# Layer 1's transposed input by way of DRAM and 32x32 transposes on VectorE instead of TensorE transposes, with its input channels in a crossed order

## The chip, the cores and the metric

The kernel runs on one core of one Trainium2 chip. A core has a matrix engine (TensorE, PE in the profile), a vector engine (VectorE, DVE), an activation engine (ScalarE, ACT), a general engine (GpSimd, POOL) and a sync engine (SP) that only issues transfers; all take their instructions in a fixed order of their own and wait for one another by semaphores. The metric is the device time of one execution in microseconds (us), lower is better. All data is 32-bit float.

## The reference

Two layers over an input `x` of 2 batches x 4096 tokens x 512 channels. Both have the same outer form: layer norm, two branches on the normalised input, both added to `x`.

```python
xn = _layernorm(x)                                  # layer 0
x = x + _L0_attn_ref(xn, ...) + _L0_ffn_ref(xn, ...)
xn = _layernorm(x)                                  # layer 1
x = x + _L1_attn_ref(xn, ...) + _L1_ffn_ref(xn, ...)

# _L0_attn_ref: x1 = xn @ w1.T; depthwise conv, silu, a state-space scan over tokens;
#               (scan * silu(xn @ v1.T)) @ w2.T
# _L0_ffn_ref:  xn and weight rounded to a 6-bit grid in blocks of 32, then xd @ wd.T
# _L1_attn_ref (linear attention):
q = relu(x @ Wq.T + bq); k = relu(x @ Wk.T + bk); v = x @ Wv.T + bv
kv = einsum('bnhd,bnhp->bhdp', k, v); k_sum = k.sum(axis=1)
out = (q @ kv) / max(q . k_sum, eps);  y = out + x;  layernorm(y) * gamma + beta
# _L1_ffn_ref, with x_prev = x one token earlier:
xr = mu_r*x + (1-mu_r)*x_prev;  xk = mu_k*x + (1-mu_k)*x_prev
sigmoid(xr @ W_r.T) * (square(relu(xk @ W_k.T)) @ W_v.T)
```

The products q, k, r and k of layer 1 contract over the channels of the normalised input. TensorE contracts over partitions, so that input must lie with channels on partitions ("transposed"), while layer norm and the values `v` use it with tokens on partitions.

## The kernel before, in words

Tokens are worked in blocks of T = 512, each of TJ = 4 tiles of 128 tokens; a batch has NB = 8 blocks, the two batches NK = 16. The program has four stages. **Stage A** (all 16 blocks) makes layer 0's two projections and the convolution. **The recurrence** runs the scan in chunks. Then for each batch come a **mixed stage** (function `mixed`, line 528), which ends layer 0 and begins layer 1, and the **layer-1 stage** (`layer1`, line 691).

In the mixed stage, `x1_of(i)` (line 576) makes the output of layer 0 for block i, called x1 here: for each tile four matmuls of the rounded branch (`branch`, line 570) and four with `w2` (line 587) go into one PSUM bank `po`, VectorE adds it to `x` (line 595), SP writes the tile to DRAM (`xd1`, line 596) for the layer-1 stage, and after the fourth tile the layer-norm scale and shift of the block stand in `mvs` (lines 600 and 601). Then for block i the loop at line 625 does the following: ScalarE writes the normalised tile `xn` (line 628); `x1_of(i + 1)` runs; sixteen TensorE transposes (four to a tile, `transposed`, line 130) go to the PSUM banks tagged `tr` and ScalarE copies them to `xnT`, channels on partitions (line 644); then for each tile a product with `wk` (line 648) into a bank tagged `mm`, VectorE's bias add (line 650), ScalarE's Relu (line 651), and one product later `summed` (line 603): `xn` against k, four matmuls of 512 columns, summed over the batch in four banks tagged `acc`. `xnT` of all eight blocks stays in SBUF for the layer-1 stage; its column 0 is the last token of the block before, copied by GpSimd (line 641).

Beside this, `gate` (line 564) loads and prepares the input `z` of block i + 2 (two transfers, a 32x32-block transpose and a multiplication on VectorE per quarter), and `quantised` (line 361) rounds tiles for the branch of later blocks: a load, four ScalarE rescales, five VectorE passes, two GpSimd passes, a VectorE transpose. `tick` (line 548) steps a clock once per tile of `x1_of` and once per tile of the k loop; it decides at which of these the four steps of a `quantised` tile are written into the program. These loads and the tiles of `gate` share eight buffers of the pool `yv`. `spread_out` (line 284) is used in stage A: it writes a block's scale and shift to DRAM and reads them back by four small transfers, so that partition 32q + p holds the values of tokens 32h + p, for all h.

The order in which an engine gets its instructions is not the order of the source: a scheduler places them when the program is built. In the built program the transposes of a block stand just ahead of its first product with `wk`.

Of the kernel before, what the change touches and what calls it, by code (L numbers as in the profile page):

```python
# [2 lines left out]

# [6 lines left out]
F32 = mybir.dt.float32  # L10
# [6 lines left out]
P = 128  # L17
D = 512
CC = D // P
T = 512  # L20
# [22 lines left out]
def block_kernel(ctx: ExitStack, tc: tile.TileContext, a: dict, out: bass.AP):  # L43
# [25 lines left out]
    q_d = dram.tile([CC, QC, L, NS, L], F32, name="q_d")  # L69
    a_d = dram.tile([CC, QC, L, NS], F32, name="a_d")  # L70
    sd = dram.tile([NK, P, TJ, 2], F32, name="sd")

    def bank(tag="mm", bufs=2):
        return ps.tile([P, D], F32, tag=tag, name=f"p_{tag}", bufs=bufs)
# [46 lines left out]
    def rescaled(dst, src, mv):  # L121
        nc.scalar.activation(dst, src, AF.Identity, bias=mv[:, 0:1], scale=mv[:, 1:2])  # L122

    def as_scale_and_bias(mv):

        nc.vector.scalar_tensor_tensor(
            mv[:, :, 0], mv[:, :, 0], -1.0, mv[:, :, 1], ALU.mult, ALU.mult
        )

    def transposed(dst, src, tag="tr"):  # L130

        pt = bank(tag).rearrange("p (c t) -> p c t", t=P)
        for cc in range(CC):
            nc.tensor.transpose(pt[:, cc, :], src[:, cc * P : (cc + 1) * P], ident)  # L134
        nc.scalar.copy(dst, pt)  # L135
# [14 lines left out]

    def laid_normalised(y, n, j):

        for h in range(QC):
            part = y.rearrange("p (c h q) -> p c h q", h=QC, q=QB)[:, :, h, :]
            rescaled(part, part, mvi[:, h, n, j, :])

    def mx_scaled(y):

# [120 lines left out]
        layernorm_stats(lambda j: xts[j], mv0[:, n])  # L281
        as_scale_and_bias(mv0[:, n])

    def spread_out(n):

        nc.sync.dma_start(out=sd[n], in_=mv0[:, n])
        for q in range(QC):
            nc.sync.dma_start(
                out=mvi[q * QB : (q + 1) * QB, :, n],
                in_=sd[n].rearrange("(h p) j k -> p h j k", p=QB),  # L290
            )

    def first_turned(work, xts):

        xnT = work.tile([P, CC, T], F32, tag="xnT", name="xnT")
# [14 lines left out]
    def turned(work, n, xi):  # L310
        xnT = work.tile([P, CC, T], F32, tag="xnT", name="xnT")
        for j in range(TJ):
            laid_normalised(xi[:, j, :], n, j)
            nc.vector.transpose(
                xnT[:, :, j * P : (j + 1) * P], xi[:, j, :].rearrange("p (c t) -> p c t", t=P)
            )
        return xnT
# [43 lines left out]
    def quantised(n, j, dst, temp):  # L361

        xq = yv.tile([P, D], F32, tag="yv", name="xq")
        nc.sync.dma_start(out=xq, in_=a["xi"][n * TJ + j])
        yield
        laid_normalised(xq, n, j)
        scales = mx_scaled(xq)
        yield
        mx_rounded(xq, scales, temp())
        yield  # L370
        nc.vector.transpose(dst().rearrange("p c t -> p (c t)"), xq)  # L371
        yield
# [155 lines left out]
    def mixed(b, z0, xds, xnTs, mvs, w2, wk):  # L528

        pg = []  # L530
        ksum = stay.tile([P, D], F32, tag="ksum", name="ksum", bufs=1)
        zs, xts, later, pos = {0: z0}, {}, [], {}
        ahead = len(xds)
        def xd_of(m, j):
            if m not in xds:
                xd = t8((P, TJ, CC, P))
                xds[m] = [xd[:, jj] for jj in range(TJ)]
            return xds[m][j]


        clock = [-2 * TJ]
        quants = [
            (2 * TJ * (m - 2) + 2 * j - 2, quantised(b * NB + m, j, partial(xd_of, m, j), t2q))
            for m in range(ahead, NB)
            for j in range(TJ)
        ]

        def tick():
            for start, q in reversed(quants):
                for t in range(start, start + 4):  # L550
                    if t == clock[0] or (t < clock[0] == -2 * TJ):
                        next(q)
            clock[0] += 1

        def x_of(i):
            xts[i] = cl.tile([P, TJ, D], F32, tag="x", name="x")
            for j in range(TJ):
                nc.sync.dma_start(out=xts[i][:, j, :], in_=tokens(x_in, b * NB + i, j))

        def flush():  # L560
            if later:
                later.pop()()

        def gate(i, cc):
            if i < NB:
                if cc == 0:
                    zs[i] = t8()
                gated(b, i, zs[i], cc)

        def branch(i, j, po):  # L570
            for k in range(CC):
                nc.tensor.matmul(  # L572
                    po, lhsT=xds[i][j][:, k, :], rhs=wd[:, k, :], start=(k == 0), stop=False
                )

        def x1_of(i):

            xt, z = xts[i], zs.pop(i)
            for j in range(TJ):
                if i in pos:  # L580
                    po = pos[i][j]
                else:
                    po = bank()
                    branch(i, j, po)
                flush()
                for k in range(CC):
                    nc.tensor.matmul(  # L587
                        po,
                        lhsT=z[:, k, j * P : (j + 1) * P],
                        rhs=w2[:, k, :],  # L590
                        start=False,
                        stop=(k == CC - 1),
                    )
                nc.gpsimd.tensor_tensor(xt[:, j, :], xt[:, j, :], b_out, ALU.add)
                nc.vector.tensor_tensor(xt[:, j, :], xt[:, j, :], po, ALU.add)  # L595
                nc.sync.dma_start(out=xd1[b * NB + i, :, j, :], in_=xt[:, j, :])
                tick()
                if i == 0:
                    gate(1, j)
            layernorm_stats(lambda j: xt[:, j, :], mvs[:, i])  # L600
            as_scale_and_bias(mvs[:, i])

        def summed(i, j, xn, kt):
            first, last = i == 0 and j == 0, i == NB - 1 and j == TJ - 1
            if first:
                pg.extend(acc() for _ in range(CC))
                nc.gpsimd.tensor_copy(ksum, kt)
            else:
                nc.gpsimd.tensor_tensor(ksum, ksum, kt, ALU.add)
            for c in range(CC):  # L610
                nc.tensor.matmul(  # L611
                    pg[c], lhsT=xn[:, j, c * P : (c + 1) * P], rhs=kt, start=first, stop=last
                )

        x_of(0)
        x_of(1)
        for i in range(ahead):

            pos[i] = [bank(("mm", "tr")[i]) if j < 2 else acc() for j in range(TJ)]
            for j in range(TJ):  # L620
                branch(i, j, pos[i][j])
                if i == 0:
                    tick()
        x1_of(0)
        for i in range(NB):
            xn = t8((P, TJ, D))
            for j in range(TJ):
                rescaled(xn[:, j, :], xts[i][:, j, :], mvs[:, i, j, :])
            if i + 2 < NB:
                x_of(i + 2)  # L630
            if i + 1 < NB:
                x1_of(i + 1)
            if i < NB - 1:
                xnT = big.tile([P, CC, T + 1], F32, tag="xnT", name="xnT")
            else:
                wide = single.tile([P, CC * (T + 1)], F32, name="wide")
                xnT = wide.rearrange("p (c t) -> p c t", t=T + 1)
            if i == 0:
                nc.gpsimd.memset(xnT[:, :, 0:1], 0.0)
            else:  # L640
                nc.gpsimd.tensor_copy(xnT[:, :, 0:1], xnTs[-1][:, :, T : T + 1])
            xnTs.append(xnT)
            for j in range(TJ):
                transposed(xnT[:, :, 1 + j * P : 1 + (j + 1) * P], xn[:, j, :])
            for j in range(TJ):
                tj = slice(1 + j * P, 1 + (j + 1) * P)
                pk = bank()
                product(pk, lambda k: xnT[:, k, tj], lambda k: wk[:, k, :])
                kt = t2("k")
                nc.vector.tensor_tensor(kt, pk, bk, ALU.add)  # L650
                nc.scalar.activation(kt, kt, AF.Relu)  # L651
                flush()
                later.append(lambda i=i, j=j, xn=xn, kt=kt: summed(i, j, xn, kt))
                gate(i + 2, j)
                tick()
        flush()
        gt = t8((P, CC, D))
        for c in range(CC):
            nc.scalar.copy(gt[:, c, :], pg[c])
        return gt, ksum  # L660
# [119 lines left out]
    with tc.tile_pool(name="tab", bufs=1) as tab:  # L780
# [3 lines left out]
        with pool("a", 2) as work, pool("pm", 1) as pm:  # L784
# [9 lines left out]
            xnT = first_turned(work, xts.pop(0))  # L794
            xts[1] = fetched(work, 1)
            measured(1, xts.pop(1))
            spread_out(1)
            xts[2] = fetched(work, 2)
            spread_out(0)
            d_ssm = column("D_ssm")  # L800
            abar, cb, b_ssm = (column(s, NS) for s in ("A", "C_ssm", "B_ssm"))
            a32 = const.tile([P, CC, L // 2], F32, name="a32")
# [16 lines left out]
            for n in range(NK):  # L819
# [4 lines left out]
                before, x1 = x1, projected(work, n, xnT, x1)  # L824
                if n + 2 < NK:
                    measured(n + 2, xts.pop(n + 2))
                    spread_out(n + 2)
                if n + 1 < NK:
                    xnT = turned(work, n + 1, xi)
                if 0 < n < NK - 1:  # L830
# [127 lines left out]
```

## Time and profile before

| | us |
|---|---|
| median of 3 runs (2497.35 to 2502.07) | 2498.64 |
| profiled execution, device time | 2500.6 |
| its span in the profile | 2498.5 |
| stage A and recurrence, up to about | 618 |
| mixed stage, batch 0, first product with `wd` to last `summed` | 618 to 1083 |
| layer-1 stage, batch 0 | 1083 to about 1557 |
| mixed stage, batch 1, its stretch in the table of stretches | 1560 to 2060 |
| layer-1 stage, batch 1 | 2060 to the end |

The profile comes from one execution. Its page gives for each engine the busy time and its share of the span; a view of the timeline lists stretches of equal instructions with their start, length and, in brackets, the idle time ahead of them and what ended it. A full-size matmul (128x128 by 128x512) appears as two passes on PE. A pass is listed as 592 ns, but the next one starts 0.43 us after it: passes overlap, so what a group of matmuls costs is read from the distance of starts, not from the sum of durations. A transpose of 128x128 is one pass.

### The profile page before, as it was taken

Reading aid. Unit: us, or ns where it says so; the run is one execution under the profiler, and the core shown is the slowest. Engines: PE = TensorE matmul, PEld = TensorE weight load, DVE = VectorE, ACT = ScalarE, POOL = GpSimd, SP = SyncE. Lnnn points to the kernel's source line nnn. Section 1 sums busy time; section 2 is a strip of 40 time slices with the busy share of each in tenths; the row PEclk is TensorE's granted clock in tenths of the full one; section 3 lists DMA queues with packets and bytes.
Section 4 is the critical chain, followed back from the end, with each engine's and each line's share of the span. In section 5 each row is a group of like instructions: output and inputs, shape, how many; then the busy total and the mean of one; then the engine's idle time right before and its main releaser. Section 6 shows DMA issues by size and latency. Waiting matters only on the chain. (4 is left out here: it accounts for less than half of the span.)

```text
span 2498.5 us, 21002 instructions
## 1 busy us (share of the span) xinstructions
PE 2444.7 (98%) x6752; PEld 1155.7 (46%) x6752; DVE 1354.6 (54%) x2796; ACT 905.5 (36%) x1668; POOL 457.7 (18%) x447
## 2 busy tenths in 40 slices
PE   7999999999999999999999999999999999999999
PEld 3444443566444444444444444444444444444444
DVE  7857465664775545126555558755542126555554
ACT  5776654444322222133333342222221133333332
POOL 1000011221443322111100003433330111100100
PEclk9999999999999999999999999999999999999999
DMA  7646332677632221101000124432220110000110
GB/s 239 214 129 213 119 117 93 180 236 249 243 114 90 84 85 68 51 33 39 34 34 34 38 72 140 157 110 91 84 85 34 51 36 36 34 34 34 38 39 25
DMA packets 168621, 239.66 MB, mean 96 GB/s; under 512 B 41408, under 2 KB 74176, under 8 KB 165440
## 3 DMA queue, kind: packets, MB, share of 16 engines
q1 hardware_dynamic: 157856, 204.77, 25.0%
q10 hardware_dynamic: 10656, 33.56, 3.4%
q8 instruction: 54, 0.88, 0.1%
q14 instruction: 55, 0.45, 0.1%
HBM read 153.77 MB, written 84.51 MB: 95 GB/s over the span
## 5 line engine op out<-in xcount | busy, mean ns | idle before, releaser
L611 PE MATMUL p_acc<-k,t 128*128 128x512 f32 x512 | 232.3, 597 | 9.2 <-ACT k L651 9.2
L140 PE MATMUL p_acc<-xnT,w_v_w 128*128 128x512 f32 x512 | 226.1, 599 | 7.8 <-ACT x L335 7.8
L750 POOL TENSOR_TENSOR x<-x,row_beta 128x512 f32<-128x512 f32 x64 | 87.8, 1372 | 794.0 <-ACT xn L122 794.0
L140 PE MATMUL p_acc<-w_W_r,t 128*128 128x512 f32 x512 | 232.8, 593 | 0.0
L140 PE MATMUL p_acc<-xnT,w_w_w 128*128 128x512 f32 x512 | 226.6, 601 | 5.8 <-DVE mv L118 5.0
L140 PE MATMUL p_mm<-t,w_W_k 128*128 128x512 f32 x512 | 222.3, 592 | 0.0
L140 PE MATMUL p_acc<-w_W_v,t 128*128 128x512 f32 x512 | 222.3, 592 | 0.0
L737 DVE TENSOR_SCALAR den<-p_tr 128x8 f32<-128x8 f32 x128 | 18.4, 151 | 348.3 <-PE p_tr L729 348.1
L140 PE MATMUL p_mm<-w_Wk,xnT 128*128 128x512 f32 x448 | 203.5, 597 | 1.6 <-DVE x L595 1.6
L587 PE MATMUL p_mm<-w_w_w,t 128*128 128x512 f32 x448 | 201.1, 592 | 0.0
L140 PE MATMUL p_mm<-xnT,w_Wq 128*128 128x512 f32 x448 | 194.8, 592 | 0.0
L572 PE MATMUL p_mm<-w_d,t 128*128 128x512 f32 x416 | 187.1, 592 | 0.2 <-DVE x L595 0.2
L122 ACT ACTIVATE xq<-xq,mvi 128x128 f32<-128x128 f32 x256 | 105.3, 482 | 204.3 <-DMA xq<-in_xi 157.4
L140 PEld LDWEIGHTS p_acc<-xnT,w_v_w 128*128 128x128 f32 x512 | 98.2, 192 | 133.1 <-issue 120.0
L140 PEld LDWEIGHTS p_acc<-xnT,w_w_w 128*128 128x128 f32 x512 | 98.4, 193 | 131.5 <-issue 121.0
L611 PEld LDWEIGHTS p_acc<-k,t 128*128 128x128 f32 x512 | 97.4, 191 | 133.2 <-issue 120.2
L140 PEld LDWEIGHTS p_mm<-t,w_W_k 128*128 128x128 f32 x512 | 97.3, 190 | 122.5 <-issue 122.2
L140 PEld LDWEIGHTS p_acc<-w_W_v,t 128*128 128x128 f32 x512 | 97.1, 190 | 121.5 <-issue 113.1
L383 DVE SCALAR_TENSOR_TENSOR xc<-x,col_conv_w,xc 128x512 f32<-128x512 f32 x128 | 92.3, 769 | 106.5 <-POOL x L325 95.3
L650 DVE TENSOR_TENSOR k<-p_mm,row_bk 128x512 f32<-128x512 f32 x64 | 43.7, 684 | 182.3 <-PE p_mm L140 182.3
L587 PEld LDWEIGHTS p_mm<-w_w_w,t 128*128 128x128 f32 x448 | 85.1, 190 | 107.1 <-issue 106.9
L140 PEld LDWEIGHTS p_mm<-xnT,w_Wq 128*128 128x128 f32 x448 | 84.8, 189 | 107.7 <-issue 107.2
(168 smaller groups left out, 3413.8 us busy)
## 6 DMA issues: line engine op xcount, KB each, us to landing
x<-in_x SPq DMA_DIRECT2D x126, 256.0 KB, 4.4
vd<-v ACTq DMA_DIRECT2D x64, 256.0 KB, 2.7
cd<-xs SPq DMA_DIRECT2D x64, 256.0 KB, 2.7
xq<-in_xi SPq DMA_DIRECT2D x64, 256.0 KB, 4.1
xg<-cd SPq DMA_DIRECT2D x16, 1024.0 KB, 7.9
v<-vd SPq DMA_DIRECT2D x64, 256.0 KB, 4.0
xd<-x SPq DMA_DIRECT2D x64, 256.0 KB, 2.3
x<-xd SPq DMA_DIRECT2D x16, 1024.0 KB, 4.7
```

Source lines behind the costliest of these rows:

```text
L122: nc.scalar.activation(dst, src, AF.Identity, bias=mv[:, 0:1], scale=mv[:, 1:2])
L140: nc.tensor.matmul(out_ap, lhsT=lhsT(k), rhs=rhs(k), start=(k == 0), stop=(k == CC - 1))
L383: nc.vector.scalar_tensor_tensor(xc, x1[:, cc, tap : tap + T], conv_w[:, cc, tap : tap + 1], xc, ALU.mult, ALU.add,)
L572: nc.tensor.matmul(po, lhsT=xds[i][j][:, k, :], rhs=wd[:, k, :], start=(k == 0), stop=False)
L587: nc.tensor.matmul(po, lhsT=z[:, k, j * P : (j + 1) * P], rhs=w2[:, k, :], start=False, stop=(k == CC - 1),)
L611: nc.tensor.matmul(pg[c], lhsT=xn[:, j, c * P : (c + 1) * P], rhs=kt, start=first, stop=last)
L650: nc.vector.tensor_tensor(kt, pk, bk, ALU.add)
L737: nc.vector.tensor_scalar(den, pc[:, :, P:], EPS_DEN, None, ALU.max)
L750: nc.gpsimd.tensor_tensor(xt[:, j, :], xt[:, j, :], beta, ALU.add)
```

## The change

The normalised x1 with channels on partitions is made without TensorE. `turned_x1(i, j)` reads the tile that was written to `xd1` back from DRAM, in four transfers of 32 partitions x 4 pieces of 128 channels, so that partition 32q + p of the buffer `y1` holds the tokens 32h + p (h = 0 to 3), of each the channels 128q to 128q + 127. Scale and shift of a token now differ by h, so ScalarE rescales `y1` in place with four instructions of 128 columns, taking the values from `mvj`, which is laid out like `y1` by `spread_out` (now a general function: one small write, four small reads per block). One VectorE transpose of 32x32 blocks writes the tile into `xnT`. Row 32q + k of chunk g of `xnT` is then channel 128q + 32g + k rather than 128g + 32q + k: a crossed order. The rows of Wq, Wk, W_r and W_k and the vectors mu_r and mu_k are laid out on the host in this order, at no cost on the device.

`xn` with tokens on partitions is still made, for `summed`. The step "load" of tile j of block i is put at tick 8i + j, which is in `x1_of(i + 1)`, and "rescale and transpose" two ticks later (the last block: four ticks earlier). `tick` now takes its steps from a table of events. The product with `wk` takes its bank from the tag `tr`, which the transposes have left, rather than `mm`. `y1` takes buffers of the pool `yv`, whose number stays eight. `transposed` remains for the first block of stage A.

```diff
+    sd1 = dram.tile([NK, P, TJ, 2], F32, name="sd1")
...
+    def spread_out(dst, via, mv):
+
+        nc.sync.dma_start(out=via, in_=mv)
+        for q in range(QC):
+            nc.sync.dma_start(
+                out=dst[q * QB : (q + 1) * QB], in_=via.rearrange("(h p) j k -> p h j k", p=QB)
+            )
...
+        clock, events = [-2 * TJ], defaultdict(list)
         def tick():
-            for start, q in reversed(quants):
-                for t in range(start, start + 4):
-                    if t == clock[0] or (t < clock[0] == -2 * TJ):
-                        next(q)
+            for do in events.pop(clock[0], ()):
+                do()
             clock[0] += 1
...
+        def xnT_of(i):
...
+        def turned_x1(i, j, mvj):
+            y = yv.tile([P, D], F32, tag="yv", name="y1")
+            for q in range(QC):
+                nc.sync.dma_start(
+                    out=y[q * QB : (q + 1) * QB].rearrange("p (h m) -> p h m", h=QC),
+                    in_=xd1[b * NB + i, :, j].rearrange("(h p) (q m) -> q p h m", h=QC, q=QC)[q],
+                )
+            yield
+            for h in range(QC):
+                part = y[:, h * P : (h + 1) * P]
+                rescaled(part, part, mvj[:, h, j, :])
+            nc.vector.transpose(
+                xnT_of(i)[:, :, 1 + j * P : 1 + (j + 1) * P].rearrange(
+                    "p g (h t) -> p h g t", h=QC
+                ),
+                y.rearrange("p (h g k) -> p h g k", h=QC, g=QC),
+            )
+            yield
...
             as_scale_and_bias(mvs[:, i])
+            mvj = stay.tile([P, QC, TJ, 2], F32, tag="mvj", name="mvj")
+            spread_out(mvj, sd1[b * NB + i], mvs[:, i])
+
+            for j in range(TJ):
+                turn = turned_x1(i, j, mvj)
+                start = 2 * TJ * i + j - (TJ if i == NB - 1 else 0)
+                at(start, partial(next, turn))
+                at(start + 2, partial(next, turn))
...
-            for j in range(TJ):
-                transposed(xnT[:, :, 1 + j * P : 1 + (j + 1) * P], xn[:, j, :])
+            xnT = xnTs[i]
             for j in range(TJ):
                 tj = slice(1 + j * P, 1 + (j + 1) * P)
-                pk = bank()
+                pk = bank("tr")
                 product(pk, lambda k: xnT[:, k, tj], lambda k: wk[:, k, :])
...
+    crossed = lambda v: v.reshape(QC, QC, QB, -1).transpose(1, 0, 2, 3).reshape(D, -1)
+    turned_crossed = lambda v: crossed(v.T)
...
-        "Wq": ("L1_attn_Wq", turned),
+        "Wq": ("L1_attn_Wq", turned_crossed),
```

## The prediction

> **What bounds the kernel now.** I read the page's busy times first:
>
> ```profile
> PE 2444.7 (98%) x6752; PEld 1155.7 (46%) x6752; DVE 1354.6 (54%) x2796; ACT 905.5 (36%) x1668; POOL 457.7 (18%) x447
> ```
>
> TensorE is the bound; nothing else is over 54%. Work taken off PE counts in full, provided what replaces it never makes PE wait. Next, the table of stretches for the two mixed stages, which the change touches (columns: stretch, length, then busy us and instructions of PE, PEld, DVE, ACT, POOL, the granted clock, DMA share, GB/s):
>
> ```profile
> 660.00:1112.00 452.00, 438.24 (x1113) 200.25 (x1113) 214.27 (x424) 114.85 (x224) 129.28 (x118) 0.99 0.24 82
> 1560.00:2060.00 500.00, 494.40 (x1275) 227.04 (x1274) 215.95 (x455) 116.48 (x224) 129.45 (x117) 1.00 0.24 81
> ```
>
> There VectorE has half its time free, ScalarE three quarters, the DMA engines three quarters. Third, PE's timeline around the sixteen transposes of block 1, which stands for the steady blocks:
>
> ```profile
> 733.56 3.60 PE L587 MATMUL p_mm<-w_w_w,t 128*128 128x512 f32 x8
> 737.00 1.04 PE L134 MATMUL p_tr<-ident,t 128*128 128x128 f32 x8
> 738.27 0.65 PE L134 MATMUL p_tr<-ident,t 128*128 128x128 f32 x4 [0.24 <-ACT xnT L135]
> 738.76 1.02 PE L140 MATMUL p_mm<-w_Wk,xnT 128*128 128x512 f32 x2
> 739.63 0.60 PE L134 MATMUL p_tr<-ident,t 128*128 128x128 f32 x4
> 740.06 6.17 PE L140 MATMUL p_mm<-w_Wk,xnT 128*128 128x512 f32 x14
> 746.07 3.60 PE L611 MATMUL p_acc<-k,t 128*128 128x512 f32 x8
> ```
>
> From 737.00 to 746.07 are 9.07 us with sixteen transposes and sixteen passes of `wk`. Eight full passes take 3.43 us from start to start (733.56 to 737.00), sixteen 6.87. The transposes with their one wait are worth **2.20 us a block**. Last, the stalls at the head of a batch, where VectorE has the rounding of several tiles at once:
>
> ```profile
> 672.17 1.12 PE L134 MATMUL p_tr<-ident,t 128*128 128x128 f32 x4 [5.31 <-ACT xnT L135]
> ...
> 699.60 3.70 PE L611 MATMUL p_acc<-k,t 128*128 128x512 f32 x8 [3.18 <-ACT k L651]
> ...
> 709.00 3.70 PE L611 MATMUL p_acc<-k,t 128*128 128x512 f32 x8 [2.27 <-ACT k L651]
> ...
> 1619.42 3.70 PE L140 MATMUL p_mm<-w_Wk,xnT 128*128 128x512 f32 x8 [1.59 <-DVE x L595]
> ...
> 1625.45 5.40 PE L611 MATMUL p_acc<-k,t 128*128 128x512 f32 x8 [2.32 <-ACT k L651]
> ```
>
> **Removed: 256 transposes.** [...] But transposes overlap as other passes do: 2.20 us for sixteen is 0.1375 us each, and the sum is 256 x 0.1375 = **35.2 us**. [...]
>
> **Added.** The rows nearest to the new operations:
>
> ```profile
> L122 ACT ACTIVATE xq<-xq,mvi 128x128 f32<-128x128 f32 x256 | 105.3, 482 | 204.3 <-DMA xq<-in_xi 157.4 <-DVE x L595 17.4 <-DMA y<-yd 7.5
> L314 DVE STREAM_TRANSPOSE xnT<-xi 128x512 f32<-128x512 f32 x60 | 38.6, 684 | 6.1 <-PE p_acc L140 3.1 <-ACT xi L122 2.9
> L390 DVE STREAM_TRANSPOSE xs<-xc 128x512 f32<-128x512 f32 x64 | 60.6, 1035 | 0.9 <-ACT xc L387 0.7
> L135 ACT COPY xnT<-p_tr 128x512 f32<-128x512 f32 x58 | 32.6, 587 | 241.3 <-PE p_tr L134 241.3
> ```
>
> - VectorE: 64 transposes. Runs of 32 elements as in L314: 0.69 us; every element apart as in L390: 1.04. I take 0.69, the nearer form: 44 us over both stages, 2.8 a block.
> - ScalarE: four rescales a tile; four of L122 take 1.65 us in the timeline, against 0.54 from start to start for the copy that goes (two in 1.08). 1.1 us more a tile, 71 us in all; ScalarE goes from 25% to about 32% of the stages, VectorE from 45% to 50%.
> - Transfers: 16.8 MB more. The nearest row for pieces of 512 bytes is `xg`, 1 MB in 7.9 us, so 16 x 7.9 = 126 us of DMA over some 950 us: from a quarter busy to under 40%.
> - SP issues per block 16 loads at 0.36 us (as `xg`), one small write at 0.34 and four small reads at 0.43: 7.8 us in 55. The twenty that it issues per block now take about as long. Each `y1` load waits for its tile of `xd1` to land (2.3 us). Behind it stand the next tile's `xd1` write, whose data comes 6.9 us later, and loads of `xq` a block ahead of need.
>
> All this lies beside PE, unless one chain is late. **The added wait** is the scale and shift by way of DRAM:
>
> ```profile
> xg<-cd SPq DMA_DIRECT2D x16, 1024.0 KB, 7.9
> ...
> xd<-x SPq DMA_DIRECT2D x64, 256.0 KB, 2.3
> ...
> mvi<-sd SPq DMA_DIRECT2D x64, 4.0 KB, 1.8
> ...
> sd<-mv SPq DMA_DIRECT2D x16, 4.0 KB, 2.7
> ```
>
> As the changed program is built, ScalarE's rescales of block m stand in its queue among the Relus of block m-1, and VectorE's first two transposes of block m among the bias adds. So a late `mvj` holds up k of the block before. I lay it on the block whose last `w2` pass ends at 851.28. `mvs` is ready 3.7 us later (L126 at 854.78); write issued and landed: 6.7; four reads issued: 8.4; landed: 10.2; sixteen rescales: 16.8; the third k's Relu behind them: 17.4. PE meanwhile has the products of tiles 0 and 1 with up to half a branch (8.6), `summed` 0 (12.0), product 2 (15.4), `summed` 1 (18.9), product 3 (22.3), and then `summed` 2, which needs that Relu. **Slack 4.9 us**: hidden. `xnT` itself is not late: tiles 0 and 1 are turned a block ahead; tiles 2 and 3 right after the first two bias adds, about 8 us before their products. The last block is turned during the k loop of block 6: its first product comes 24.9 us after its `x1` ends, the chain takes about 13.
>
> **Moved.** The products with `wk` go to the `tr` banks: `po` and `pk` no longer share two banks, which removes the 1.59 us at 1619.42. GpSimd's copy of column 0 moves ahead, into `x1_of`; behind it stand the products of the rounding, and GpSimd is at 28% there, so nothing. The layer-1 stages and all before 618 us keep their order: nothing.
>
> **Head of a batch.** In batch 0, `mvs` comes at 662.8. With the chain above (small reads landing near 670, rescale, transpose), the first product starts near 672.5, against 673.08 now; before it PE runs part of the branch of block 2, which it does later now. But four more transposes (2.8 us) stand in VectorE's queue, which is full there, ahead of the late k. Bounds: all waits of this head go (5.3 + 3.2 + 2.3 = 11 us gained), or VectorE's extra work and a wait behind ScalarE come on top (4 lost). I take 1 gained, nearest to a shift of the same queue. In batch 1: 1.6 from the bank, the rest as now, since the Relu of tile 0 still waits for the same rounding; bounds 6 and -3; I take 1.
>
> **Sum.** 35.2 + 1 + 1 = 37 us off the profiled execution's 2500.6 (span 2498.5 and 2.1 around it): 2463.6. The profiled execution lies 2 us over the median of the runs, 2498.64; the forecast for the median is **2462**, within 2454 to 2470.
>
> **Rivals.**
> 1. *More*: the head stalls nearly vanish (11 + 6 us, as PE has branch work to fill them and its own banks), giving 2498.6 - 35 - 17 = **2446**. For it: the bank wait. Against: what limits there is VectorE, which gets more to do. 10%.
> 2. *Half*: in-order waiting on ScalarE or VectorE (rounding behind turns, turns behind rounding) costs PE about 1.2 us in each of 16 blocks: 2498.6 - 37 + 19 = **2481**. For it: the queues of both hold waits on transfers where they held waits on PE. Against: the slack above. 20%.
> 3. *No change*: stalls of just the size of the gain, or the rescheduled program loses elsewhere: **2499**. 5%.
> 4. *Slower*: the chain by way of DRAM is twice as long (6.5 us more, as SP sits in front of a `y1` load that waits for a buffer of `yv`; the trace has SP waiting up to 25 us for one). [...] For it: sixteen buffers' worth of loads per block on eight buffers. Against: as built, those loads stand before the small write in the queue, 7 us apart. 10%.
>
> The main case has 55%. Faster by over 0.2% (5 us; less can't be told from no change here): main, more and half, 85%, of which I take off 1 since half can go further. Same 5%, slower 11%. The range 2446 to 2487 leaves out the two last rivals and the far end of half.
>
> **What would show it.** No transposes on TensorE after the first 20 us. PE busy about 72 us lower by listed durations, but the span only some 37. Steady blocks 54.9 us apart instead of 57.1. If PE shows waits on ScalarE's k in steady blocks, rival 2 or 4; if those waits lead back to the small reads, 4. A VectorE transpose near 1.04 us, or small reads landing over 15 us after `mvs`, would make the forecast wrong.

## The result, and the profile after

The changed kernel takes 2502.89 us (median of 14 runs, 2498.72 to 2508.13), the kernel before, in the same measurement, 2500.09 (14 runs, 2497.35 to 2503.6). The ratio is 1.001, with a 95% interval of 1.0002 to 1.0018: no gain, by the bound of 0.2% no change. Both profiled executions have a span of 2498.5 us. The forecast was 2462.

The page after (busy us, share of the span, instructions):

```profile
PE 2424.0 (97%) x6496; PEld 1131.4 (45%) x6496; DVE 1393.4 (56%) x2860; ACT 970.7 (39%) x1860; POOL 458.9 (18%) x447
```

The 256 transposes are gone (6752 to 6496), and PE is busy 20.7 us less, yet the span is the same. The table of stretches, for the same two rows and columns as before (the mixed stage of batch 1 ends at 2020 us, where PE takes up `Wq`, and not at 2060, so 40 us of the second row belong to the layer-1 stage):

```profile
660.00:1112.00 452.00, 427.53 (x993) 188.73 (x992) 233.56 (x462) 147.37 (x322) 130.41 (x117) 0.98 0.32 102
1560.00:2060.00 500.00, 483.86 (x1139) 214.67 (x1138) 234.43 (x481) 148.65 (x318) 129.56 (x116) 0.98 0.31 96
```

The first column after the length is PE: it now stands still for 24.5 us in the first stretch (13.8 before) and 16.1 in the second (5.6 before), and the clock is 0.98, not 0.99 and 1.00. Nothing is saturated: in the first stretch VectorE has 52%, ScalarE 33%, DMA 32%. So PE waits. Its timeline at a steady block (block 3 of batch 0):

```profile
855.57 4.45 PE L150 MATMUL p_tr<-w_Wk,xnT 128*128 128x512 f32 x10
859.86 1.88 PE L613 MATMUL p_mm<-w_d,t 128*128 128x512 f32 x4
863.58 2.84 PE L150 MATMUL p_tr<-w_Wk,xnT 128*128 128x512 f32 x6 [1.84 <-DVE xnT L588]
866.26 3.60 PE L660 MATMUL p_acc<-k,t 128*128 128x512 f32 x8
```

A product with `wk` is eight passes, two per chunk of `xnT`. The ten passes are product 0 and chunk 0 of product 1. Then PE has a piece of the branch to do, and stands still for 1.84 us until a VectorE transpose (L588) ends: chunk 1 of product 1, which needs tile 1. VectorE at that time:

```profile
814.22 0.71 DVE L588 STREAM_TRANSPOSE xnT<-y 128x512 f32<-128x512 f32 x1 [0.83 <-ACT y L124]
...
854.04 0.69 DVE L172 TENSOR_REDUCE mx_s<-xq 128x16 f32<-128x512 f32 x1 [3.50 <-ACT xq L124]
...
857.97 0.68 DVE L636 TENSOR_TENSOR x<-x,p_mm 128x512 f32<-128x512 f32 x1
...
862.26 0.65 DVE L691 TENSOR_TENSOR k<-p_tr,row_bk 128x512 f32<-128x512 f32 x1
862.83 0.69 DVE L588 STREAM_TRANSPOSE xnT<-y 128x512 f32<-128x512 f32 x1
```

The reader is to see two things. The transpose that releases PE at 863.5 stands behind k's bias add of tile 0: it is that of **tile 2**, not of tile 1. Tiles 0 and 1 were turned in the block before, as soon as ScalarE had rescaled them; 814.22 is tile 1. And all of VectorE's queue is late: the last `x` add (L636) could have run when `w2` ended at 855.57, but starts at 857.97, behind a rounding step that waited 3.50 us for `xq`. SP's queue tells why `xq` is late (each row is an issue; L637 writes an x1 tile, L580 reads it back as `y1`):

```profile
844.96 0.34 SPq L637 DMA_DIRECT2D xd<-x  x1
847.21 1.73 SPq L580 DMA_DIRECT2D y<-xd  x4
848.98 0.43 SPq L365 DMA_DIRECT2D xq<-in_xi  x1
```

The four `y1` loads wait until the tile that they read has landed in DRAM, 1.9 us after SP was done with the write, and their issue takes 1.73 us more. The load of `xq`, which waits for nothing of the kind, is held up behind both. The heads of the batches got longer too (batch 0; at the second row the profile names `mvs`, but VectorE's transpose of 746.22 ends at the same moment):

```profile
704.27 6.10 PE L660 MATMUL p_acc<-k,t 128*128 128x512 f32 x8 [6.04 <-ACT k L692]
...
746.97 4.38 PE L150 MATMUL p_tr<-w_Wk,xnT 128*128 128x512 f32 x6 [8.27 <-DVE mvs L113]
```

Where the time went, stretch by stretch, from the starts of PE's groups ("head" runs from the first product with `wd` to the k product of block 3, in the kernel before to its transposes; "rest" from there on). The bounds are 617.65, 851.28, 1083.29, 1557.09 and 1789.61 us before, 614.34, 855.57, 1080.65, 1553.61 and 1793.67 after. The last two columns are two of the experiments below:

| stretch, us | before | after | forecast change | measured change | e4_noturn | e5_poolq |
|---|---|---|---|---|---|---|
| to the first product with `wd` | 617.7 | 614.3 | 0 | -3.4 | 615.4 | 617.4 |
| head, batch 0 | 233.6 | 241.2 | -7.6 | +7.6 | 235.7 | 228.8 |
| rest of the mixed stage, batch 0 | 232.0 | 225.1 | -11.0 | -6.9 | 222.5 | 220.6 |
| layer-1 stage, batch 0 | 473.8 | 473.0 | 0 | -0.8 | 473.8 | 473.0 |
| head, batch 1 | 232.5 | 240.1 | -7.6 | +7.6 | 228.6 | 230.2 |
| rest, batch 1, to the end | 708.9 | 704.8 | -11.0 | -4.1 | 698.4 | 699.2 |
| span | 2498.5 | 2498.5 | -37.2 | 0 | 2474.3 | 2469.2 |

(Forecast: three of the blocks' transposes lie in a head, five in a rest, 2.2 us each, and 1 us for each head.) The first row is no part of the change; it lay between 614 and 620 us in all runs. The gain was made in the rests and given back in the heads, and even in the rests only half of it came. Where in the rests it came is telling:

```profile
912.61 4.46 PE L150 MATMUL p_tr<-w_Wk,xnT 128*128 128x512 f32 x10
...
969.91 4.46 PE L150 MATMUL p_tr<-w_Wk,xnT 128*128 128x512 f32 x10
...
1024.84 4.45 PE L150 MATMUL p_tr<-w_Wk,xnT 128*128 128x512 f32 x10
```

Block 4 takes 57.30 us, block 5 the forecast 54.93, with nothing in the program altered. VectorE has no `xq` to reduce (L172) between 935 and 1043 us: the loss stops where the rounding of the batch stops.

### The profile page after: what moved, and what is told of

Read it like the earlier page. It is cut to its first block, busy times and chain, and to the rows that moved or that the text cites. A ratio compares the mean times of both kernels' runs of the same rounds, so it can differ in the third digit from the quotient of the medians.

```text
span 2498.5 us, 21351 instructions
## 1 busy us (share of the span) xinstructions
PE 2424.0 (97%) x6496; PEld 1131.4 (45%) x6496; DVE 1393.4 (56%) x2860; ACT 970.7 (39%) x1860; POOL 458.9 (18%) x447
## 5 line engine op out<-in xcount | busy, mean ns | idle before, releaser
L150 PE MATMUL p_tr<-w_Wk,xnT 128*128 128x512 f32 x448 | 213.8, 622 | 29.9 <-DVE xnT L588 17.4
L150 PEld LDWEIGHTS p_tr<-w_Wk,xnT 128*128 128x128 f32 x448 | 88.3, 200 | 147.3 <-issue 106.5
```

The source lines that it names most:

```text
L150: nc.tensor.matmul(out_ap, lhsT=lhsT(k), rhs=rhs(k), start=(k == 0), stop=(k == CC - 1))
```

## Experiments

Two explanations are tested. **F**, a false wait: product 1 waits for the write of tile 2, because the four pieces of that write, 513 columns apart, span the addresses of tile 1's chunks 1 to 3. **Q**, the queues: `y1` loads hold `xq` back on SP, `xq` holds VectorE back. All ratios are to the kernel before, run beside.

### Moving the turn in time: e1_early and e2_late

All blocks but the first turned four ticks earlier:

```diff
-                start = 2 * TJ * i + j - (TJ if i == NB - 1 else 0)
+                start = 2 * TJ * i + j - (TJ if i else 0)
```

> All blocks but the first are turned four ticks earlier, as the last block is already (load, rescale and transpose of a tile alike); nothing else changes. Theory F (false wait): in the changed kernel TensorE stops in each block at the second matmul of the second k product, because the VectorE transpose of tile 2 stands ahead of that product in the program and writes an address range that spans the later chunks of tile 1; it has nothing to do with tile 1's own data. With all four transposes written ahead of the block's products they are done a block early, the waits of the k products on the transposes go in the steady blocks, block starts lie 54.9 us apart instead of 57.1, and the time is 2466 to 2478. Theory L (load): VectorE and ScalarE have too much to do in the mixed stage, and TensorE waits for them wherever the transposes are put: the waits move to the x adds or the Relus, block starts stay near 57 us, 2496 to 2508.

Measured: 2483.88 us, ratio 0.9934 (0.9919 to 0.9949), between the two ranges. What was gained lies in the heads (228.2 us in batch 0 and 232.9 in batch 1, for 241.2 and 240.1). The wait in product 1 is gone from the steady blocks, but these still take 56 to 59 us. The timeline of PE at block 3:

```profile
842.69 7.03 PE L150 MATMUL p_tr<-w_Wk,xnT 128*128 128x512 f32 x16
851.84 5.40 PE L660 MATMUL p_acc<-k,t 128*128 128x512 f32 x8 [2.12 <-ACT k L692]
```

Products 0 and 1 run through, and then PE waits for k: its bias add is late, because the last `x` add came 3.37 us after `w2` ended, again behind a rounding step that had waited 2.30 us for `xq`. The wait had moved, its source had not.

Rescale and transpose of tiles 2 and 3 one tick **later**, behind the product of the tile before:

```diff
-                at(start + 2, partial(next, turn))
+                at(start + 2 + (0 if i == NB - 1 else j // 2), partial(next, turn))
```

> The rescale and transpose of tiles 2 and 3 (not in the last block) are put one tick LATER than in the changed kernel, so that each stands in the program behind the k product of the tile before it. Theory F: product 1 no longer stands behind the transpose of tile 2, so its inner wait goes although the transpose comes later; product 2 and 3 have their own transposes about 3 us ahead of need, behind the summed product of the tile before. Most of the 35 us comes, 2466 to 2480. Theory L, or a true wait for tile 1's data: the later transpose makes the wait longer, 2502 to 2515.

Measured: 2493.64 us, ratio 0.9976 (0.997 to 0.9983), again between the two ranges. Block 3, PE's and VectorE's timelines:

```profile
856.24 7.03 PE L150 MATMUL p_tr<-w_Wk,xnT 128*128 128x512 f32 x16
864.77 3.70 PE L660 MATMUL p_acc<-k,t 128*128 128x512 f32 x8 [1.50 <-ACT k L692]
```

```profile
858.84 0.68 DVE L636 TENSOR_TENSOR x<-x,p_mm 128x512 f32<-128x512 f32 x1
...
865.48 0.69 DVE L588 STREAM_TRANSPOSE xnT<-y 128x512 f32<-128x512 f32 x1
```

Products 0 and 1 run through and are over at 863.3; tile 2 is turned only at 865.48, 9.2 us into the block (7.3 in the changed kernel). So product 1 never needed what it waited for: **the false wait is shown**. That the span of the write is its reason is argued: chunk 0 of tile 1, which lies outside the span, was not waited for. But the false wait is not the whole loss. VectorE's last add is as late as before (2.6 us after `w2` ended), PE now waits 1.50 us for k instead, and blocks 2 to 4 still take 56.6 to 57.0 us. Without Q cured, the wait moves on.

### The bank and the whole turn: e3_mm and e4_noturn

```diff
-                pk = bank("tr")
+                pk = bank()
```

> The changed kernel with the k products back in the banks tagged mm, which they share with the output of layer 0; the tr banks then serve only the first blocks. Tells what the move of the banks is worth. Both theories: the waits on the transposes stay, and waits on the x add come on top where VectorE is late, 1 to 2 us a block in some blocks: 2502 to 2520. If the banks don't matter: 2499 to 2506.

Measured: 2525.66 us, ratio 1.0103 (1.008 to 1.0125), slower than was expected. With the products in the `mm` banks as before, VectorE is as late as in the changed kernel (last add 2.30 us after `w2`, 2.40 there), but the branch passes that filled PE's time between products 0 and 1 are missing, and PE waits 3.45 us at block 3 rather than 1.84. The move of the bank is worth some 23 us to this kernel; the forecast had counted it at 1.6.

```diff
-            for h in range(QC):
-                part = y[:, h * P : (h + 1) * P]
-                rescaled(part, part, mvj[:, h, j, :])
-            nc.vector.transpose(
...
+            xnT_of(i)
...
-            mvj = stay.tile([P, QC, TJ, 2], F32, tag="mvj", name="mvj")
-            spread_out(mvj, sd1[b * NB + i], mvs[:, i])
+            mvj = None
```

(`xnT` is set to a constant; the `y1` loads go as well.)

> The changed kernel without its turns: no reading back of x1, no mvj, no rescale of y1, no transpose on VectorE; GpSimd fills each xnT with a constant instead (128 x 2052, some 2 us a block). It measures what the removal of TensorE's transposes is worth when what replaces them costs nothing. By the prediction's sum 35 us plus what the head of a batch gains: both theories 2450 to 2466. If the time stays above 2480, the transposes were not worth 35 us to begin with.

Measured: 2477.17 us, ratio 0.9907 (0.9892 to 0.9922), above the 2450 to 2466 expected. Without any turn the steady blocks are 54.9 us apart, so what was removed is worth the forecast 2.2 us a block; but the heads give 2.1 us back in batch 0 and gain 3.9 in batch 1, against 7.6 forecast for each. Batch 0 is no clean measure: six of the fills with the constant, 1.8 us each, stand on GpSimd between 632 and 652 us, ahead of rounding passes. In batch 1 all fills come before the head. In both heads PE waits for k with no turn in the way:

```profile
709.64 5.20 PE L642 MATMUL p_acc<-k,t 128*128 128x512 f32 x8 [5.67 <-ACT k L674]
...
1615.23 6.37 PE L642 MATMUL p_acc<-k,t 128*128 128x512 f32 x8 [5.90 <-ACT k L674]
```

The bias add of that k stands in VectorE's queue among rounding steps; from 690 to 710 us VectorE is busy for 16.3 of 20 us. That VectorE's load sets the pace there is read from this, not tested.

### The cut transpose and the queue: e8_split and e5_poolq

Meant as F alone, with nothing moved: the transpose of a tile cut into four, each writing one contiguous piece.

```diff
-            nc.vector.transpose(
-                xnT_of(i)[:, :, 1 + j * P : 1 + (j + 1) * P].rearrange(
-                    "p g (h t) -> p h g t", h=QC
-                ),
-                y.rearrange("p (h g k) -> p h g k", h=QC, g=QC),
-            )
+            for g in range(QC):
+                nc.vector.transpose(
+                    xnT_of(i)[:, g, 1 + j * P : 1 + (j + 1) * P].rearrange(
+                        "p (h t) -> p h t", h=QC
+                    ),
+                    y.rearrange("p (h g k) -> p h g k", h=QC, g=QC)[:, :, g, :],
+                )
```

> The changed kernel with each VectorE transpose of a tile cut into four, one per chunk of xnT, so that each writes one contiguous piece of 128 columns. Same data, same moment, more instructions (192 more on VectorE, some 0.2 us each instead of one of 0.70, about +0.1 to 0.2 us a tile). Theory F (the product of tile 1 waits for the transpose of tile 2 only because the address span of one covers the other): that wait is gone without anything being moved in time; steady blocks near 55.5 to 56.5 us, wait ended by VectorE's transpose below 0.5 us a block outside the heads, about 2487 us. Rival Q (VectorE is simply late: its queue is held up by the rounding and by the add of the last tile): the same lateness stops PE at tile 2's product or at summed, and the time stays within 4 us of the changed kernel's 2503.

Measured: 2484.61 us, ratio 0.994 (0.9923 to 0.9956). From block 2 on the blocks are 54.93 us apart, and PE's wait is gone. But something did move. Block 3, the timelines of PE and of VectorE:

```profile
853.05 7.03 PE L150 MATMUL p_tr<-w_Wk,xnT 128*128 128x512 f32 x16
...
863.35 3.60 PE L150 MATMUL p_tr<-w_Wk,xnT 128*128 128x512 f32 x8
```

```profile
853.76 0.68 DVE L637 TENSOR_TENSOR x<-x,p_mm 128x512 f32<-128x512 f32 x1
...
863.55 0.89 DVE L589 STREAM_TRANSPOSE xnT<-y 128x128 f32<-128x128 f32 x4 [2.75 <-ACT y L124]
```

The eight passes of 863.35 are product 2, which reads tile 2, and they start before the first transposes of this stretch (863.55, as soon as ScalarE has rescaled). So these are of the next block, and tile 2 of this one was turned a block ahead, like tiles 0 and 1. A likely reason is the same span the other way round: in one piece the write of tile 2 covers chunks that product 0 still reads. No run tests that. VectorE's last add is 0.7 us behind `w2`, not 2.4. So the run shows that the cut gives the steady blocks their gain, but not by which part: it took away the false wait, the late place of tiles 2 and 3, and with them most of VectorE's lateness. The time is outside Q's range, yet Q is not refuted by a run in which the lateness went too. What is missing to 2462 lies in the heads.

Q alone: the changed kernel with the `y1` loads on GpSimd's queue.

```diff
-                nc.sync.dma_start(
+                nc.gpsimd.dma_start(
```

> The changed kernel with the y1 loads issued by GpSimd's queue instead of SP's. Theory S (loads of y1 that wait for their tile of xd1 hold back on SP the loads of xq and y of later blocks, which makes VectorE late): xq comes earlier, VectorE's idle time behind ScalarE's rescale of xq falls, and a part of the loss goes: about 2490 us. Theory F (false wait alone): PE still waits for the transpose of tile 2, 2498 to 2503 us. Rival G (a load that waits blocks GpSimd as it did SP, and GpSimd's rounding passes and ksum come late): slower than the changed kernel, 2508 us or more.

Measured: 2471.89 us, ratio 0.9889 (0.9874 to 0.9904); with e12_late_poolq, below, the fastest version found. The false wait is still in the program, but VectorE is on time. Block 3, in SP's, VectorE's and PE's timelines:

```profile
826.82 8.74 SPq L637 DMA_DIRECT2D xd<-x  x2
835.66 0.38 SPq L365 DMA_DIRECT2D xq<-in_xi  x1
```

```profile
846.40 0.69 DVE L636 TENSOR_TENSOR x<-x,p_mm 128x512 f32<-128x512 f32 x1 [0.87 <-PE p_mm L628]
...
851.19 0.69 DVE L588 STREAM_TRANSPOSE xnT<-y 128x512 f32<-128x512 f32 x1
```

```profile
846.20 4.45 PE L150 MATMUL p_tr<-w_Wk,xnT 128*128 128x512 f32 x10
850.49 1.88 PE L613 MATMUL p_mm<-w_d,t 128*128 128x512 f32 x4
852.21 2.74 PE L150 MATMUL p_tr<-w_Wk,xnT 128*128 128x512 f32 x6
```

`xq` is issued 10.5 us ahead of the block instead of 6.6, the add follows `w2` at once and is released by PE itself, and tile 2 is turned at 851.88, 0.3 us before PE comes to chunk 1 of product 1. So in the steady blocks **Q is the cause**, and the false wait is the way by which it reaches PE: with VectorE on time the false wait costs nothing (here, and in block 5 of the changed kernel), and with VectorE late but the false wait gone the time is lost at k (e1_early, e2_late). The edit takes from SP both the waiting of the `y1` loads and the time of their issue; at block 3 the two were of about the same size (1.9 and 1.73 us), and no run separates them.

### The dose from the other side: e10_xq_poolq

The `y1` loads stay on SP, the `xq` loads go to GpSimd's queue.

```diff
-        nc.sync.dma_start(out=xq, in_=a["xi"][n * TJ + j])
+        nc.gpsimd.dma_start(out=xq, in_=a["xi"][n * TJ + j])
```

> The complement of e5_poolq: the y1 loads stay on SP, and the loads of xq (the rounding's input) go to GpSimd's queue instead. If what the y1 loads hold back on SP is above all xq, and through it the rounding and VectorE's in-order queue, the late add of the last tile is early again: steady blocks near 55 us, 2470 to 2478 us. If it is other loads behind them (y, v and x, the small scale reads, the next xd1 write): PE's waits for the transpose stay, 2495 to 2503 us.

Measured: 2533.41 us, ratio 1.0135 (1.012 to 1.015), outside both expectations, because I had not asked what would stand ahead of `xq` on GpSimd: its rounding passes and `ksum`, which wait for VectorE and ScalarE (between 828 and 858 us the rounding passes up to 6.06 us for VectorE, `ksum` 4.31 and 2.06 us for ScalarE). `xq` is issued later still (858.38, 5.7 us ahead of the block). As an experiment on the cause it serves all the same, with the dose raised. VectorE, then PE, at block 3:

```profile
863.69 0.69 DVE L172 TENSOR_REDUCE mx_s<-xq 128x16 f32<-128x512 f32 x1 [4.83 <-ACT xq L124]
...
868.35 0.68 DVE L636 TENSOR_TENSOR x<-x,p_mm 128x512 f32<-128x512 f32 x1
```

```profile
873.87 4.54 PE L150 MATMUL p_tr<-w_Wk,xnT 128*128 128x512 f32 x6 [3.60 <-DVE xnT L588]
```

The four kernels at this block, us from the start of its first product, in the kernel before of its transposes (differences of starts in the timelines; VectorE, then PE, in the kernel before):

```profile
842.87 0.65 DVE L162 TENSOR_REDUCE mx_s<-xq 128x16 f32<-128x512 f32 x1
...
851.49 0.69 DVE L595 TENSOR_TENSOR x<-x,p_mm 128x512 f32<-128x512 f32 x1 [2.02 <-PE p_mm L587]
```

```profile
851.28 1.04 PE L134 MATMUL p_tr<-ident,t 128*128 128x128 f32 x8
...
908.43 1.04 PE L134 MATMUL p_tr<-ident,t 128*128 128x128 f32 x8
```

| | `xq` reduced | last `x` add | tile 2 turned | PE's wait in product 1 | to the next block |
|---|---|---|---|---|---|
| before | -8.4 | 0.2 | (none) | (none) | 57.15 |
| e5_poolq | -5.9 | 0.2 | 5.0 | 0 | 54.93 |
| after | -1.5 | 2.4 | 7.3 | 1.84 | 57.04 |
| e10_xq_poolq | -0.4 | 4.2 | 9.0 | 3.60 | 61.63 |

Later `xq`, later add, later turn, longer wait, in step.

### Both cures, and the heads: e6, e9, e9b, e11, e12

e6_early_poolq joins the edits of e1_early and e5_poolq.

> The turn four ticks earlier (as in e1_early) and the y1 loads on GpSimd's queue. If what is left in e1_early (PE waits at summed 0 for k, whose bias add stands behind a rounding step that waits for xq) comes from SP's queue: PE's waits for k in steady blocks go, 55 us a block, about 2473 us. If GpSimd is blocked instead by the waiting loads: 2484 us or slower. If it is VectorE's order alone, whatever issues the loads: 2481 to 2486.

Measured: 2472.14 us, ratio 0.989 (0.9876 to 0.9905), steady blocks 55.12 us. The waits for k in steady blocks, which e1_early had kept, are gone: they were Q. It is no better than e5_poolq.

e9_split_early_poolq adds the cut of e8_split to it, e9b_split_poolq adds that cut to e5_poolq.

> All three: transposes cut by chunk, four ticks earlier, y1 loads on GpSimd's queue. If the false wait is still paid somewhere in e6_early_poolq, this one is faster by some us; if the earlier place had taken it away in full, the two agree within 3 us, or this is slower by the added VectorE instructions (up to 4 us).

> e5_poolq with the transposes cut by chunk, so without the false wait. In steady blocks both should be at 54.9 us, since either cure alone reached it. If the false wait still costs in the heads, where PE in e5_poolq waits 7.1 us (batch 0 stretch) for VectorE's transpose: about 2465 us. If the heads are bound by VectorE's queue, which gets three more instructions a tile: 2472 to 2484.

Measured: 2483.12 us (0.9934, 0.9919 to 0.9949) and 2475.32 (0.9905, 0.9889 to 0.9922). The cut now costs: 11 us more than e6_early_poolq, beyond the 4 that were allowed, and about 3 more than e5_poolq. Four small transposes take 0.89 us a tile (863.55 above) for 0.70, which is 12 us of VectorE over 64 tiles; in e9_split_early_poolq the steady blocks take 56.23 us, mostly with a wait of 1.03 us for k. With the queue mended, the false wait costs nothing that a cut could win back.

e12_late_poolq joins e2_late and e5_poolq.

> e5_poolq with rescale and transpose of tiles 2 and 3 one tick later, behind the product of the tile before, as in e2_late. Without the false wait in the way and without the late queue, the steady blocks stay at 54.9 us or lose up to 1 us to a true wait for tile 2. In the heads the first product's second chunk no longer waits for tile 2's transpose: if that counts there, some 4 us off, about 2468; if the wait only moves to the next product, 2472 to 2478.

Measured: 2470.16 us, ratio 0.9885 (0.987 to 0.99), not to be told from e5_poolq. Steady blocks 54.93; the wait of the first blocks only moved.

e11_q4_poolq puts the rounding two ticks earlier in e5_poolq:

```diff
-                    at(2 * TJ * (m - 2) + 2 * j - 2 + step, partial(next, q))
+                    at(2 * TJ * (m - 2) + 2 * j - 4 + step, partial(next, q))
```

> e5_poolq with the rounding of every later tile put two ticks (half a block) earlier in the program. What is still missing against the forecast of 2462 lies in the heads, where the rounding of the third and fourth block stands among the first bias adds and transposes. If that order on VectorE makes the heads slow: one head gets shorter by up to 5 us each, about 2463. If the heads are full whatever the order (the same work has to be done there, and now sooner): 2472 or slower, with longer waits for k in the first block.

Measured: 2504.46 us, ratio 1.0022 (1.0015 to 1.0029). All 33 us of e5_poolq are lost again: blocks 2 to 4 take 57 to 60 us, with waits of 1.1 to 6.7 us for the transpose of tile 2 and, in the heads, up to 6.1 for k, as VectorE now has rounding where it should turn. The heads got longer (240 us each, for 229 and 230). So e5_poolq has no margin to spare, and its remaining 10 us to the forecast are not settled by these runs. They lie in the heads; e4_noturn points to VectorE's load there, and what order would relieve it stays open.

## Why the prediction was wrong

**What held.** The transposes were worth 2.2 us a block: in e4_noturn, e5_poolq and e8_split the steady blocks go from 57.14 to 54.93. The distance of starts was thus the right measure; the listed duration (mean 280 ns) would have made it 4.5. My expectation that PE's busy time would fall by 72 us by listed durations (256 of 280 ns) was a slip of that kind: busy time counts an overlap once, the kernel before has those 256 transposes busy for 37.2 us, and e5_poolq shows 2414.7, 30 us less. The costs that were added were sized right, as these rows say (the source view of L588, ns min/median/max; the list of transfers, KB and us to landing):

```profile
L588 DVE STREAM_TRANSPOSE xnT<-y x56: 668/702/714, 668.8 to 1973.6; 128x512 f32<-128x512 f32 x56
```

```profile
y<-xd SPq DMA_DIRECT2D x256, 64.0 KB, 2.1
...
mvj<-sd SPq DMA_DIRECT2D x64, 4.0 KB, 1.7
```

The transpose took 0.70 us (0.69 taken), over the two stretches ScalarE went to 31% (32%), VectorE to 49% (50%), the small reads landed in 1.7 us (1.8). The chain by way of DRAM, on which the slower rival rested, was hidden: no wait in a steady block of the changed kernel leads back to it.

**The step that failed** is in the paragraph on the added wait: "tiles 2 and 3 right after the first two bias adds, about 8 us before their products", and so "`xnT` itself is not late". The place in the queue was right, the time and the reader were not. First, it was measured from an undelayed VectorE. In the same text I had noted that each `y1` load waits for its tile to land and that "loads of `xq` a block ahead of need" stand behind it, and had let the lead of a block cover it. The lead was not a block: at block 3 the rounding of that `xq` stands ahead of the last `x` add on VectorE, and 3.95 us of delay on SP (from 10.5 to 6.6 us ahead of the block; `xq` stood behind the waiting and the issue of four `y1` loads) came out as 2.2 us on that add and 2.3 us on the turn. Second, the turn of tile 2 is waited for not by product 2 but already by chunk 1 of product 1, which does not need it. For that reader little of the 8 us was left: in e5_poolq, the undelayed case, tile 2 is ready 0.3 us before PE comes to it. In place of blocks of 54.9 us came blocks of 57.0 to 59.0, as long as the rounding lasted. That all losses together come to just the gain is chance; no step of the sum led there.

**The heads** were the second error, of size and sign: +7.6 us each instead of -7.6. Set against the 6.6 us of their transposes, that is a loss of 14.2 us in each, which I had bounded at 4 and 3. They have the most rounding for VectorE (37 of the 51 reductions of `xq` in the two mixed stages of the changed kernel), and the same late `xq`; e5_poolq turns them to -4.8 and -2.3, so most of the loss is Q. The rest seems to be that a gain on PE is not a gain where VectorE sets the pace: e4_noturn, with no turn at all, gets +2.1 and -3.9 there.

**The clock.** A stall had no one price. In blocks 2 to 4 of the two batches the changed kernel's PE waits six times, 1.84 to 2.23 us. Twice the six passes behind the gap took 4.54 us for 2.74, four times they lost 0.1: 4.0 us in all. At the price of the row of before at 1625.45 us (2.32 us idle, then eight passes in 5.40 us for 3.60, so 1.8 lost) it would be 10.8. In the rival's sum, "half" by in-order waiting named the right mechanism ("rounding behind turns, turns behind rounding") at 1.2 us a block; with the false wait, the clock and the heads it was about twice that, which ends at no change.

That the transposes went to VectorE is not what decided: with its loads on another queue the same change makes the kernel 1.1% faster (e5_poolq).

## What to carry to other kernels

A load that waits for a write to DRAM held back what stood behind it on its issuing queue (1.9 us at block 3), and so did the time of its own issue (1.73 us for four): before putting one there, list what stands behind it and who, on an engine that works in order, stands behind that. Where a tile is written in strided pieces, ask which parts of its neighbours lie inside the span of the write: here the reader of such parts waited 1.84 us at block 3 for data that it did not need, and that the span is the reason was argued, not tested. A gain on the bound engine is worth counting only in stretches where no other engine sets the pace (without any turn, and so without 6.6 us of transposes in each, the heads changed by +2.1 and -3.9 us), and slack should be reckoned from the reader that the built program has, not from the one that needs the data (of some 8 us 0.3 were left at block 3 of e5_poolq).

## What the runs showed of the hardware

What a gap on PE cost the passes behind it did not follow from its length alone. Two blocks of the changed kernel:

```profile
1802.08 2.84 PE L150 MATMUL p_tr<-w_Wk,xnT 128*128 128x512 f32 x6 [2.23 <-DVE xnT L588]
...
1859.34 4.54 PE L150 MATMUL p_tr<-w_Wk,xnT 128*128 128x512 f32 x6 [2.06 <-DVE xnT L588]
```

The longer gap cost 0.1 us, the shorter one 1.8; the granted clock over the six passes was 1.00 behind the longer and 0.61 behind the shorter. In e10_xq_poolq a gap of 3.61 us cost 0.1 as well, and one of 3.60 cost 1.8. Taking all groups of six or more full-size passes in the two mixed stages (from 600 to 1110 and from 1530 to 2080 us) of all fourteen traces, by their length over that of such a group without a gap: behind each of the 43 gaps of 1 to 1.89 us 0.1 us was lost; of the 35 gaps of 1.91 to 3.61 us twelve cost 0.1 and the others 0.4 to 3.0; behind each of the 41 gaps of 3.62 to 10.24 us 1.5 to 3.0 were lost. These are the gaps that these kernels happen to have, no run varied one alone, and what decides between 0.1 and 1.8 is not shown. The stall of 2.06 us came to 3.9 us with what the passes behind it lost.

A `y1` load's issue took 0.55 to 0.57 us on GpSimd's queue (e5_poolq, around block 3), on SP 0.43 (median of 256). GpSimd's busy time went from 458.9 us in the changed kernel to 593.8 in e5_poolq, from 18% to 24% of the span.
